# Linear attention and a gated FFN, 16 blocks of tokens: the first and last block's transpose moved from TensorE to VectorE squares and DMAs, with three steps reordered around it

## The chip, the cores and the metric

One core of a Trainium2 chip. The time is device microseconds of one execution. Beside the times there is one profiled execution, and its trace is what the profile views below come from. All clock times in this document (for example "44.55") are microseconds from the start of the span of the kernel that is named.

## What is computed

The input x is 4 x 2048 tokens of 256 features, float32. An attention without softmax, in chunks of 32 tokens, is followed by a gated FFN with integer weights; each is added to its input, and each sum is normalized.

```python
Q, K, V = x @ W_q.T, x @ W_k.T, x @ W_v.T
S = einsum('bncd,bnkd->bnck', Qc, Kc) * mask        # chunks of 32 tokens; decay ** (i - j) below the diagonal
O = einsum('bnck,bnkd->bncd', S, Vc).reshape(B, T, D)
out = sigmoid(x @ W_g.T) * O @ W_o.T + x
h = layernorm(x + out)
u = silu(h @ wg.T) * (h @ wu.T)                     # wg, wu, wd: integers / 127; hidden size 768
result = layernorm(h + u @ wd.T)
```

## The kernel before, in words

The 8192 tokens are cut into 16 blocks of 512 (`NB` = 16, `TB` = 512); a block has 4 groups (`NG`) of 128 tokens. A block goes through these steps, each a function:

- `attn_gate` (L295), `attn_y` (L311), `attn_v` (L327): products with weights from xT, the input with features on partitions. y is x times W_q.T W_k, so that scores are y times x. ScalarE takes the gate's sigmoid (L308) and copies v (L343); VectorE copies y (L324).
- `attn_scores` (L348): scores of chunks, masked by VectorE (L366); `attn_values` (L371): scores times v, times the gate (L384, goT).
- `attn_out` (L411): product with W_o (L396, tile pa), residual (L417), and `layer_norm` (L276): moments (L261, L262) and scaling (L281 to L285) on VectorE, the root (L270) on ScalarE. The result h is multiplied by 2**23 (`H_UP`).
- The transpose of h to features on partitions, as a float32r high part (hT_hi) and a float16 rest (hT_lo). Two ways exist. `transpose_h` (L425) does it on TensorE: 8 transposes of 128x128 into two PSUM banks (L433, tile pt), a ScalarE activation for the high part (L436), a VectorE operation for the rest (L437). `move_h` (L444) transposes 32x32 squares on VectorE (L451, tile sq, 4 instructions) and moves the squares to their places with 16 DMAs of 32 KB on the sync engine's queue SP (L457, tile hT); `split_h` (L465) then makes the two parts from SBUF, on ScalarE (L474) and VectorE (L475), kept in program order on their engines.
- `ffn_up` (L482): six chunks of 128 hidden units. A chunk is 8 matmuls of 512 columns into two banks (L492, tiles fg and fu); in even chunks the high parts go first, in odd ones the low parts. Then ScalarE's sigmoid s (L500), two VectorE products (L501, L503, tile u), and u split into u_hi on ScalarE (L510) and u_lo on GpSimd (L511).
- `ffn_down` (L513): 48 matmuls for a block (L396, tile fdn), 12 for each group of tokens, a high and a low part for each of six chunks; residual (L518). `finish` (L530) normalizes and stores.

Blocks 0 and 1 start the pipeline. In the loop (L569), turn b does the attention of block b + 2 and the FFN of block b: y, gate, v and scores of b + 2; `move_h` of block b + 1; three chunks of the FFN of b; the values of b + 2; `split_h` of b + 1; three more chunks; `attn_out` of b + 2; `ffn_down` of b. So blocks 1 to 14 are transposed by squares and DMAs, with a turn's work between the move and the first use. Block 0 and block 15 use `transpose_h`: block 0 before the loop (L564), block 15 in the tail after the loop (L604), in the middle of block 14's FFN. After the loop come block 14's FFN and block 15's, the latter in two halves of 256 tokens so that its end is short.

The engines work through their queues in order. A scheduler fixes these orders when the program is built, from the program's order, its own estimates and the buffers: eight PSUM banks in rotation, two buffers for most working tiles, and one each for sq and hT (the pool `moved`), so that a block's squares wait until the former block's DMAs have read theirs.

Of the kernel before, what the change touches and what calls it, by code (L numbers as in the profile page):

```python
# [48 lines left out]
TB = 512  # L49
NG = TB // P  # L50
SCALE = 1.0 / 127.0
EXACT = 2048.0
H_UP = 2.0**23
# [5 lines left out]
def kernel(  # L59
# [25 lines left out]
    work = ctx.enter_context(tc.tile_pool(name="work", bufs=2))  # L85
# [8 lines left out]
    def bank(name):  # L94
        return psum.tile([P, TB], F32, tag="ps", name=name)
# [180 lines left out]
    def layer_norm(dst, r, name, on_r=1.0, on_dst=1.0):  # L276


        mv = moments(r, name)
        rstd = root(mv, name, on_r)  # L280
        nc.vector.reciprocal(rstd, rstd)  # L281
        if on_dst != on_r:
            nc.vector.tensor_scalar(rstd, rstd, on_dst / on_r, None, ALU.mult)  # L283
        for g in range(NG):
            nc.vector.tensor_scalar(  # L285
                dst[:, g, :],
                r[:, g, :],
                mv[:, g, 0:1],
                rstd[:, g : g + 1],
                ALU.subtract,  # L290
                ALU.mult,
            )
# [55 lines left out]
    def attn_scores(b, yT):  # L348
        xt = xTs.pop(b)
        halves = [slice(i * PAIR, (i + 1) * PAIR) for i in range(P // PAIR)]  # L350
        ps = bank(f"ps_{b}")[:, : NG * PAIR].rearrange("p (g c) -> p g c", c=PAIR)
        for g in range(NG):
            for fc in range(KD):
                for rows in halves:
                    tokens = slice(g * P + rows.start, g * P + rows.stop)
                    nc.tensor.matmul(  # L356
                        ps[rows, g, :],
                        lhsT=xt[:, fc, tokens],
                        rhs=yT[:, fc, tokens],
                        start=(fc == 0),  # L360
                        stop=(fc == KD - 1),
                    )
# [45 lines left out]
    def flat(t, gs):  # L408
        return t[:, gs, :].rearrange("p g d -> p (g d)")

    def attn_out(b, goT, up=H_UP):  # L411
        xn = xns.pop(b)
        r = norm.tile([P, NG, D], F32, tag="h", name=f"h_{b}")

        def residual(gs, pb):

            nc.vector.scalar_tensor_tensor(  # L417
                flat(r, gs), flat(xn, gs), 2.0, pb, ALU.mult, ALU.add
            )

        project_back(b, (chunked(goT),), wo, KD, residual, "pa")
        layer_norm(r, r, f"a{b}", on_dst=up)
        return r

    def transpose_h(b, h, up=H_UP):  # L425

        up = H_UP / up
        hi = work.tile([P, KD, TB], F32R, tag="hT_hi", name=f"hT_hi_{b}")
        lo = work.tile([P, KD, TB], F16, tag="hT_lo", name=f"hT_lo_{b}")
        for dc in range(KD):  # L430
            pt = bank(f"pt_{b}_{dc}")
            for g in range(NG):
                nc.tensor.transpose(  # L433
                    pt[:, g * P : (g + 1) * P], h[:, g, dc * P : (dc + 1) * P], ident
                )
            nc.scalar.mul(hi[:, dc, :], pt, up)  # L436
            nc.vector.scalar_tensor_tensor(  # L437
                lo[:, dc, :], pt, up, hi[:, dc, :].bitcast(F32), ALU.mult, ALU.subtract
            )
        return hi, lo  # L440

    NQ = P // SQ

# [104 lines left out]
    goT = attn_values(first, sT, v, sg)  # L548
    if second:
        sT_second = attn_scores(second, ys.pop(second))  # L550
    hs[first] = attn_out(first, goT, 1 if NB == 1 else H_UP)
    fg, fu = (
        [integers(w, name, dtype) for dtype in (F32R, F16)]
        for w, name in zip(ffn_int, ("fg", "fu"))
    )
    if second:
        goT = attn_values(second, sT_second, v_second, sg_second)
    if NB > 2:
        xTs[2] = load_xT(2)
        ys[2] = attn_y(2)  # L560
    if second:
        hs[second] = attn_out(second, goT, 1 if NB == 2 else H_UP)
    fd = integers(ffn_int[2], "fd", F32R)
    hTs[first] = transpose_h(first, hs[first], 1 if NB == 1 else H_UP)  # L564


    half = range(KH // 2), range(KH // 2, KH)
    looked = 0
    for b in range(NB - 2):  # L569
        n = b + 2  # L570
        if n not in xTs:
            xTs[n] = load_xT(n)
        xns[n] = load_xn(n)
        hT = hTs.pop(b)
        uT = [], []
        yT = ys.pop(n) if n in ys else attn_y(n)
        sg, v = attn_gate(n), attn_v(n)
        sT = attn_scores(n, yT)
        moving = move_h(b + 1, hs[b + 1])
        ffn_up(b, hT, uT, half[0])  # L580
        goT = attn_values(n, sT, v, sg)
        hTs[b + 1] = split_h(b + 1, moving)
        ffn_up(b, hT, uT, half[1])
        hs[n] = attn_out(n, goT, 1 if n == NB - 1 else H_UP)
        finish(b, ffn_down(b, uT, hs.pop(b)))
        if looked < len(halves):
            look_up(looked)
            looked += 1
# [12 lines left out]
    if NB > 1:  # L601
# [192 lines left out]
```

## Time and profile before

| | us |
|---|---|
| three runs | 554.58, 554.70, 552.32 (median 554.58) |
| profiled execution | 552.7 |
| its span, first to last instruction | 550.9 |
| granted TensorE clock, mean | 0.997 |
| TensorE busy | 541.8 (98% of the span) |
| VectorE, ScalarE, GpSimd busy | 385.7, 230.1, 128.7 |
| one turn of the loop (75.32 to 108.72) | 33.40 |
| 8 transposes on TensorE in the chain, twice | 0.87 each time |
| 16 DMAs of a move, first issue to last issue's end (50.45 to 60.78) | 10.33 |

A line of the timeline reads: start, length, engine, line of the code, operation, output <- inputs, shapes, number of instructions merged; in brackets the idle time of the engine before it and what ended that. The chain of waits goes back from the last instruction, at each step to what released it, or to the instruction before it on its engine; its rows are start, length, engine and line. A list of waits has the engine and line that waited, the one waited for, and the total, the number and the longest of the waits. The trace's stages: start of the pipeline to about 53, then 14 turns to about 509, then the tail; the last matmuls of the FFN's chunks end near 538, and normalization and stores take the rest.

### The profile page before, as it was taken

The page shows a single profiled execution, that of the slowest core. Times are in us where ns is not written, and L with a number is a line of the kernel's source. Part 1 is how long each engine was busy: PE and PEld are TensorE (multiplying, and loading weights), DVE is VectorE, ACT ScalarE, POOL GpSimd, SP SyncE. Part 2 cuts the span into 40 slices and gives each one's busy share as a digit, 9 for nine tenths or more (in the row PEclk, how much of TensorE's full clock was granted, in tenths as well). Part 3 has the DMA queues.
Part 4 walks back from the last instruction along what each step waited for, and adds up shares of the span by engine and source line. Part 5 has one row for each costly group of instructions (what it writes and reads, how often), then busy time and mean ns, then how long its engine had stood idle before and what let it go on. Part 6 is the DMA issues. An engine that isn't in the chain of part 4 may idle for free.

```text
span 550.9 us, 8470 instructions
## 1 busy us (share of the span) xinstructions
PE 541.8 (98%) x3150; PEld 396.6 (72%) x3150; DVE 385.7 (70%) x956; ACT 230.1 (42%) x382; POOL 128.7 (23%) x122
## 2 busy tenths in 40 slices
PE   8999999999999999999999999999999999999994
PEld 5577777867668686677857778676676866778694
DVE  4276885859668486894848758496784858848874
ACT  2226524335243352533435243452433425344755
POOL 2000402205022040311305022050221403123453
PEclk9999999999999999999999999999999999999998
DMA  8431223121221312214121231213213120020102
GB/s 266 161 109 52 65 60 95 39 73 43 90 64 39 97 53 65 56 44 111 39 66 50 75 80 39 75 42 93 61 39 91 63 62 16 6 72 1 38 2 80
DMA packets 41996, 36.77 MB, mean 67 GB/s; under 512 B 4576, under 2 KB 37344, under 8 KB 41952
## 3 DMA queue, kind: packets, MB, share of 16 engines
q1 hardware_dynamic: 40832, 35.15, 22.2%
q10 hardware_dynamic: 1088, 1.05, 0.6%
q8 instruction: 26, 0.43, 0.3%
q14 instruction: 18, 0.15, 0.1%
q0 software_dynamic: 32, 0.00, 0.0%
HBM read 20.45 MB, written 8.39 MB: 52 GB/s over the span
## 4 chain that ended last, share of the span: by engine, by line
PE 97%; DMA 1%; ACT 1%; DVE 1%; issue 0%; POOL 0%; DVEq 0%
PE fg L492 16%; PE fu L492 16%; PE fdn L396 16%; PE pa L396 10%; PE pv L336 10%; PE pg L301 10%; PE py L317 10%; PE po L377 5%; PE ps L356 3%; DMA wg<-in_w_gT_dram 1%; ACT r L635 0%; PE pt L433 0%; PE pm L159 0%; ACT L270 0%; ACT rstd_f L270 0%
## 5 line engine op out<-in xcount | busy, mean ns | idle before, releaser
L511 POOL TENSOR_TENSOR u_lo<-u,u_hi 128x512 fp32r<-128x512 f32 (+1 forms) x102 | 123.9, 1216 | 412.1 <-ACT u_hi L510 407.7
L500 ACT ACTIVATE s<-fg 128x512 f32<-128x512 f32 (+1 forms) x102 | 58.1, 570 | 76.9 <-PE fg L492 76.9
L396 PE MATMUL fdn<-fd_hi,u_hi 128*128 128x256 f32 x360 | 89.1, 290 | 0.0
L396 PE MATMUL fdn<-fd_hi,u_lo 128*128 128x256 f32 x360 | 86.5, 282 | 0.0
L501 DVE TENSOR_TENSOR s<-fg,s 128x512 f32<-128x512 f32 (+1 forms) x102 | 66.7, 654 | 27.7 <-ACT s L500 27.6
L510 ACT CAST u_hi<-u 128x512 fp32r<-128x512 f32 (+1 forms) x102 | 60.4, 592 | 48.2 <-DVE u L503 48.1
L503 DVE TENSOR_TENSOR u<-fu,s 128x512 f32<-128x512 f32 (+1 forms) x102 | 67.3, 660 | 13.6 <-POOL u_lo L511 1.0
L492 PE MATMUL fg<-hT_hi,fg_hi 128*128 128x512 f32 (+1 forms) x204 | 71.4, 431 | 0.0
L366 DVE TENSOR_TENSOR sT<-ps,mask 64x256 f32<-64x256 f32 x32 | 13.5, 422 | 79.9 <-PE ps L356 79.7
L396 PEld LDWEIGHTS fdn<-fd_hi,u_lo 128*128 128x128 f32 x360 | 67.9, 189 | 0.4
L396 PEld LDWEIGHTS fdn<-fd_hi,u_hi 128*128 128x128 f32 x360 | 67.8, 189 | 0.4
L492 PE MATMUL fu<-hT_hi,fu_hi 128*128 128x512 f32 (+1 forms) x204 | 61.5, 382 | 0.0
L492 PE MATMUL fg<-hT_lo,fg_lo 128*128 128x512 f16 (+1 forms) x204 | 58.7, 369 | 0.0
L336 PEld LDWEIGHTS pv<-wv,xT 128*128 128x128 f32 x256 | 48.6, 190 | 13.4 <-issue 7.7
L492 PE MATMUL fu<-hT_lo,fu_lo 128*128 128x512 f16 (+1 forms) x204 | 58.1, 366 | 0.0
L301 PE MATMUL pg<-xT,wg 128*128 128x512 f32 x128 | 57.6, 593 | 0.3 <-DMA wg<-in_w_gT_dram 0.3
L396 PE MATMUL pa<-wo,goT 128*128 128x256 f32 x256 | 58.0, 379 | 0.0
L336 PE MATMUL pv<-wv,xT 128*128 128x256 f32 x256 | 57.9, 379 | 0.0
L317 PE MATMUL py<-xT,m_sb 128*128 128x512 f32 x128 | 57.6, 593 | 0.0
L396 PEld LDWEIGHTS pa<-wo,goT 128*128 128x128 f32 x256 | 48.5, 190 | 7.6 <-DVE rstd_a L283 0.2
L301 PEld LDWEIGHTS pg<-xT,wg 128*128 128x128 f32 x128 | 24.2, 190 | 31.0 <-issue 25.6
L492 PEld LDWEIGHTS fg<-hT_hi,fg_hi 128*128 128x128 f32 x204 | 36.6, 189 | 10.3
(90 smaller groups left out, 625.2 us busy)
## 6 DMA issues: line engine op xcount, KB each, us to landing
x<-in_x_dram SPq DMA_DIRECT2D x16, 512.0 KB, 3.6
xT<-in_xT_dram SPq DMA_DIRECT2D x15, 512.0 KB, 3.9
out_dram<-r SPq DMA_DIRECT2D x15, 512.0 KB, 3.3
hT<-sq SPq DMA_DIRECT2D x224, 32.0 KB, 1.9
fg_int<-in_ffn_gT_dram SPq DMA_DIRECT2D x1, 768.0 KB, 9.2
fu_int<-in_ffn_uT_dram SPq DMA_DIRECT2D x1, 768.0 KB, 10.6
fd_int<-in_ffn_dT_dram SPq DMA_DIRECT2D x1, 768.0 KB, 11.0
xT<-in_xT_dram SPq DMA_DIRECT2D x2, 256.0 KB, 4.4
```

Source lines behind the costliest of these rows:

```text
L301: nc.tensor.matmul(pg, lhsT=wg[:, ec, dc * P : (dc + 1) * P], rhs=xt[:, ec, :], start=(ec == 0), stop=(ec == KD - 1),)
L317: nc.tensor.matmul(py, lhsT=m_sb[:, ec, fc * P : (fc + 1) * P], rhs=xt[:, ec, :], start=(ec == 0), stop=(ec == KD - 1),)
L336: nc.tensor.matmul(pv[:, j * D : (j + 1) * D], lhsT=xt[:, ec, g * P : (g + 1) * P], rhs=wv[:, ec, :], start=(ec == 0), stop=(ec == KD - 1),)
L356: nc.tensor.matmul(ps[rows, g, :], lhsT=xt[:, fc, tokens], rhs=yT[:, fc, tokens], start=(fc == 0), stop=(fc == KD - 1),)
L377: nc.tensor.matmul(po[:, cols], lhsT=v[:, g, dc * P : (dc + 1) * P], rhs=sT[:, cols], start=True, stop=True,)
L396: nc.tensor.matmul(pb[:, j * D : (j + 1) * D], lhsT=part[k][:, g * P : (g + 1) * P], rhs=w[:, k, :], start=(i == 0), stop=(i == len(terms) ...
L492: nc.tensor.matmul(pb, lhsT=w[kind][:, dc, hc * P : (hc + 1) * P], rhs=hT[kind][:, dc, cols], start=(kind == kinds[0] and dc == 0), stop=( ...
L500: nc.scalar.activation(s, pg, AF.Sigmoid, scale=SCALE / H_UP)
L501: nc.vector.tensor_tensor(s, pg, s, ALU.mult)
L503: nc.vector.tensor_tensor(u, pu, s, ALU.mult)
L510: nc.scalar.copy(hi, u)
L511: nc.gpsimd.tensor_tensor(lo, u, hi.bitcast(F32), ALU.subtract)
```

## The change

`transpose_h` goes, and with it the option of `attn_out` to leave h unscaled: every block's h carries the factor 2**23 and is transposed by `move_h` and `split_h`. Around this:

- Block 0: `move_h` right after its `attn_out`; `split_h` in the first turn, after the scores of block 2.
- The input xT of block 3 is loaded with that of block 2, and block 3's y is made in the first turn, between the scores of block 2 and the first chunk of block 0's FFN, no longer in block 1's turn.
- Block 1: `split_h` after all six chunks of block 0's FFN, no longer in their middle.
- Block 15: in the last turn (b = 13), `attn_out` is done after four chunks of block 13's FFN instead of six (the variable `late` holds the other two), then `move_h` of block 15, the two late chunks, the first two chunks of block 14's FFN (`ahead`), and then block 13's `ffn_down`. In the tail come chunks 2 to 4 of block 14, a ScalarE multiplication that takes the factor out of block 15's h (128x1024), `split_h` of block 15, and chunk 5.

```diff
-    def attn_out(b, goT, up=H_UP):
+    def attn_out(b, goT):
...
-        layer_norm(r, r, f"a{b}", on_dst=up)
+        layer_norm(r, r, f"a{b}", on_dst=H_UP)
...
-    def transpose_h(b, h, up=H_UP):
...
-    hs[first] = attn_out(first, goT, 1 if NB == 1 else H_UP)
+    hs[first] = attn_out(first, goT)
+    moving = move_h(first, hs[first])
...
+    for b in range(2, min(NB, 4)):
+        xTs[b] = load_xT(b)
     if NB > 2:
-        xTs[2] = load_xT(2)
         ys[2] = attn_y(2)
...
-    hTs[first] = transpose_h(first, hs[first], 1 if NB == 1 else H_UP)
...
+    ahead = half[0][: 2 if NB > 2 else 0]
+    uTs = {}
...
-        hT = hTs.pop(b)
-        uT = [], []
+        uT = uTs.pop(b, ([], []))
         yT = ys.pop(n) if n in ys else attn_y(n)
         sg, v = attn_gate(n), attn_v(n)
         sT = attn_scores(n, yT)
+        if b == first:
+            hTs[b] = split_h(b, moving)
+            if n + 1 < NB:
+                ys[n + 1] = attn_y(n + 1)
+        hT = hTs.pop(b)
         moving = move_h(b + 1, hs[b + 1])
         ffn_up(b, hT, uT, half[0])
         goT = attn_values(n, sT, v, sg)
-        hTs[b + 1] = split_h(b + 1, moving)
-        ffn_up(b, hT, uT, half[1])
-        hs[n] = attn_out(n, goT, 1 if n == NB - 1 else H_UP)
+        if b != first:
+            hTs[b + 1] = split_h(b + 1, moving)
+
+        late = half[1][1:] if n == NB - 1 else half[1][:0]
+        ffn_up(b, hT, uT, half[1][: len(half[1]) - len(late)])
+        if b == first:
+            hTs[b + 1] = split_h(b + 1, moving)
+        hs[n] = attn_out(n, goT)
+        if n == NB - 1:
+            moving = move_h(n, hs[n])
+            ffn_up(b, hT, uT, late)
+            uTs[b + 1] = [], []
+            ffn_up(b + 1, hTs[b + 1], uTs[b + 1], ahead)
         finish(b, ffn_down(b, uT, hs.pop(b)))
...
-        uT = [], []
-        ffn_up(last - 1, hTs[last - 1], uT, half[0])
-        hTs[last] = transpose_h(last, hs[last], 1)
-        ffn_up(last - 1, hTs[last - 1], uT, half[1])
+        uT = uTs.pop(last - 1, ([], []))
...
+        ffn_up(last - 1, hTs[last - 1], uT, range(len(ahead), KH - 1))
+        plain = flat(hs[last], slice(0, NG))
+        nc.scalar.mul(plain, plain, 1 / H_UP)
+        hTs[last] = split_h(last, moving)
+        ffn_up(last - 1, hTs[last - 1], uT, range(KH - 1, KH))
```

More of the change, by code (lines that the diff above doesn't have):

```diff
@@ L421, in attn_out @@
         project_back(b, (chunked(goT),), wo, KD, residual, "pa")
-        layer_norm(r, r, f"a{b}", on_dst=up)
+        layer_norm(r, r, f"a{b}", on_dst=H_UP)
         return r
-    def transpose_h(b, h, up=H_UP):
[L427 to L440, printed above, removed]
     NQ = P // SQ
@@ L557 @@
         goT = attn_values(second, sT_second, v_second, sg_second)
+    for b in range(2, min(NB, 4)):
+        xTs[b] = load_xT(b)
     if NB > 2:
-        xTs[2] = load_xT(2)
         ys[2] = attn_y(2)
     if second:
-        hs[second] = attn_out(second, goT, 1 if NB == 2 else H_UP)
+        hs[second] = attn_out(second, goT)
     fd = integers(ffn_int[2], "fd", F32R)
-    hTs[first] = transpose_h(first, hs[first], 1 if NB == 1 else H_UP)
     half = range(KH // 2), range(KH // 2, KH)
+    ahead = half[0][: 2 if NB > 2 else 0]
+    uTs = {}
     looked = 0
@@ L600 @@
     early = range(0)
-    if NB > 1:
-        uT = [], []
-        ffn_up(last - 1, hTs[last - 1], uT, half[0])
-        hTs[last] = transpose_h(last, hs[last], 1)
-        ffn_up(last - 1, hTs[last - 1], uT, half[1])
+    if NB == 1:
+        hTs[last] = split_h(last, moving)
+        plain = flat(hs[last], slice(0, NG))
+        nc.scalar.mul(plain, plain, 1 / H_UP)
+    else:
+        uT = uTs.pop(last - 1, ([], []))
+        if NB == 2:
+            hTs[last - 1] = split_h(last - 1, moving)
+            moving = move_h(last, hs[last])
+        ffn_up(last - 1, hTs[last - 1], uT, range(len(ahead), KH - 1))
+        plain = flat(hs[last], slice(0, NG))
+        nc.scalar.mul(plain, plain, 1 / H_UP)
+        hTs[last] = split_h(last, moving)
+        ffn_up(last - 1, hTs[last - 1], uT, range(KH - 1, KH))
         early = half[0]
```

## The prediction

> **What bounds the kernel now.** I read the busy shares first, then who waits, then the chain of waits, at both ends of the span. The page's first part and the chain's shares:
>
> ```profile
> PE 541.8 (98%) x3150; PEld 396.6 (72%) x3150; DVE 385.7 (70%) x956; ACT 230.1 (42%) x382; POOL 128.7 (23%) x122
> ...
> PE 97%; DMA 1%; ACT 1%; DVE 1%; issue 0%; POOL 0%; DVEq 0%
> ```
>
> TensorE is the bound in every stage but the last 13 us. TensorE's list of waits has two rows, both at the start:
>
> ```profile
> PE pi L145 <- DVE idle L142: 1.5, 1, 1.5
> PE pg L301 <- DMA wg<-in_w_gT_dram: 0.3, 1, 0.3
> ```
>
> So nothing in the middle can be won by shortening a wait: a gain needs TensorE work to go, and any new wait of TensorE is a loss of its full length. The work that goes, in the chain (start, length):
>
> ```profile
> 41.09 3.45 PE pa L396 x16
> 44.55 0.87 PE pt L433 x8
> 45.42 3.44 PE pg L301 x8
> 48.86 3.45 PE pv L336 x16
> 52.31 1.08 PE ps L356 x32
> ...
> 514.58 0.87 PE pt L433 x8
> ```
>
> What replaces it is the path by which blocks 1 to 14 already go. In the timeline, the first such move (block 1):
>
> ```profile
> 47.70 1.38 DVE L285 TENSOR_SCALAR h<-h,mv_a,rstd_a 128x256 f32<-128x256 f32 x4
> 49.00 1.42 DVE L451 STREAM_TRANSPOSE sq<-h 128x256 f32<-128x256 f32 x4
> 50.45 10.33 SPq L457 DMA_DIRECT2D hT<-sq  x16
> 62.07 1.14 ACT L474 CAST hT_hi<-hT 128x512 fp32r<-128x512 f32 x2 [0.68 <-DMA hT<-sq]
> ```
>
> The reader is to see 11.65 us from the end of the transposes (50.42) to the first hT_hi (62.07), 10.3 of it the issue of 16 DMAs one behind the other. A TensorE transpose takes 0.87; this takes 13 with the squares. It is free only under 13 us of other TensorE work.
>
> **What the Trainium skill says.** "VectorE: DVE Perf Modes", section "The three transpose paths": only TensorE and the DMA crossbar do a full 128x128; VectorE does 32x32 blocks, hence the DMAs. It gives 390 ns for one on TensorE (bf16); here eight f32 ones add 870 ns to the chain, 109 each. [...]the trace has 1.9 us median from issue to landing (1.8 to 3.6). "ScalarE: Activation LUTs", "What ACT_TABLE_LOAD costs": 1283 ns plus a drain of 1380. The trace has 1.28, and the next operation starts 0.01 later (539.47 to 540.76), so I use 1.28 alone. "TensorE: Matmul & The Clock Gate", Part 1: the clock falls after an idle window of some 3.4 us; the granted clock is 0.997 here, and no wait below is that long, so I add nothing for it.
>
> **The change part by part.** The instruction queues of the built program agree with the ones before from block 1's turn to the middle of block 13's (block 3's y apart): only the two ends change. Times are in the clock of the profiled execution before.
>
> *Removed:* 16 transposes, 2 x 0.87 = 1.74 us, all on the path.
>
> *Start.* Block 2's gates now start at 44.55, so gates, v and scores end at 44.55 + 3.44 + 3.45 + 1.08 = 52.52. Block 3's y (3.43) stands there now instead of in block 1's turn: its cost is moved, not added. Block 0's first chunk may start at 55.95. Its data: the normalization L285 of block 0 starts at 40.43; as in the rows above, transposes start 1.30 later and last 1.42, so 43.15; plus 11.65 is 54.80; two casts at 0.53 to 0.6 give hT_hi at 55.4 and 55.95, just in time. ScalarE, with an additional pair of table loads between the two gate sigmoids (2 x 1.28), is free at 54.25 by its queue: covered by 0.5. VectorE decides. The buffer of the squares is single, so block 1's squares wait for block 0's 16 DMAs (54.80), and three of them (1.07) and a copy of y (0.65) are queued ahead of hT_lo: 56.5, then 0.65 each, 57.15 and 57.8. TensorE wants hT_lo at 55.95 + 2 x 0.47 = 56.9 and would be through with the gate's low pair at 57.35; now 57.8 + 0.22 = 58.0. **New wait S = 0.7.** From both sides: 0 if the DMAs are issued at the 0.585 that is the shortest in the trace (0.9 earlier), 2.4 if the last lands after 3.6 instead of 1.9. No gain is possible, since the work is unchanged.
>
> On SP's queue the 16 DMAs pass ahead of block 3's x (about 53.6 instead of 45.3; it is read some 50 us later) and of block 4's xT: nothing. Block 1's own move starts near 59.4 and lands near 71; its chunks start near 87: 16 us of cover. In block 1's turn TensorE has 3.43 less work ahead of block 2's split: landing some 15 us after the down projection, read at 16; only ScalarE would wait, and the next reader on TensorE is a turn away. Nothing.
>
> *End.* A chunk is 1.80 (three in 60.77 to 66.17). Block 15's output product moves from 499.95 to 496.35, ending 499.80; its goT is ready at 495.73, covered by 0.6. Then follow chunks 4 and 5 of block 13 (to 503.40), chunks 0 and 1 of block 14, and the down projection of block 13 from 507.1. The rows before for its last chunk's cover:
>
> ```profile
> 501.29 0.69 DVE L503 TENSOR_TENSOR u<-fu,s 128x512 f32<-128x512 f32 x1
> ...
> 502.01 0.62 ACT L510 CAST u_hi<-u 128x512 fp32r<-128x512 f32 x1 [0.80 <-DVE u L503]
> ...
> 502.71 1.29 POOL L511 TENSOR_TENSOR u_lo<-u,u_hi 128x512 fp32r<-128x512 f32 x1
> ```
>
> After the chunk's matmuls (499.95) the low part is ready at 504.0, used at 504.56. Now block 15's normalization and four transposes stand ahead of chunk 5 on VectorE: residual and moments 499.05 to 502.3 (3.25, as at 468.55), chunk 4's two products to 503.8, reciprocal and scaling to 504.15, normalization and squares 1.30 + 1.42 to 506.87, then s of chunk 5, s of the next, u of chunk 5: 508.75. Cast 0.62, GpSimd 1.29: high part 509.4, low part 510.7. The program has put these two terms at places 18 and 23 of the projection, at 0.12 each: wanted at 509.15 and, 0.6 later, 510.0. **New wait A = 1.0**; 0 if VectorE's queue runs 1 us shorter, 2.5 if the terms stood in their old places (11 and 12) or the queue is 1.5 longer. The rescaling of h (128x1024; an estimate of 1.1, twice a 128x512 activation of 0.59) ends near 508.0 on ScalarE, 0.75 ahead of the cast.
>
> Let E be the projection's end. Block 15's DMAs, from 506.9, land near 518.5; E is about 513.9 and its split comes at E + 6.5: covered by 1.9. But the split's VectorE half stands behind chunk 4 of block 14. Before, the second chunk after the projection had its u at 515.56, E + 6.39 (two table loads, block 13's normalization and chunk before it). So now chunk 3's u is at E + 6.4, chunk 4's at E + 7.8, hT_lo at E + 9.05 and 9.65. TensorE has four chunks, 7.2 us, and 0.46 of high parts: it wants hT_lo at E + 7.66. **New wait B = 1.5**, from 0.5 to 2.6 (two VectorE products more or fewer). Then chunk 5's u, behind two products, is at E + 11.35, its low part at E + 13.3; block 14's projection starts at E + 7.2 + 1.5 + 2.75 (three half chunks, 520.85 to 523.60) = 11.45 and wants it eleven matmuls later, 12.8: **C = 0.5**, from 0 to 1. The last 13 us are as before.
>
> **Sum:** -1.74 + 0.7 + 1.0 + 1.5 + 0.5 = **+2.0 us**. Span 550.9 to 552.9; the profiled execution 552.7 to 554.7. The three runs before are 552.32, 554.58 and 554.70, so executions fall near 552.5 or near 554.6; I add 2.0 to the mean of all four, 553.6: **555.6**. Against the median of 554.58 that is within 0.5%, which is about what a measurement of this kernel can tell from no change.
>
> **The rivals.** *The covers hold* (chance 0.22): hT_lo and u_lo come as fast as the shortest rows allow, waits total 0.7 or less: -1.0, 552.6. For it: each wait hangs on less than 1.5 us. Against: VectorE is 89% busy from 500 to 521 already (18.71 of 21.00), and its order is fixed. *VectorE at the end becomes the bound* (0.28), and it ends slower: normalization, squares and split of block 15 all lie in VectorE's queue ahead of products that TensorE needs, so A, B and C near their upper ends, 2.5 + 2.6 + 1.0, with S 0.7: 6.8 - 1.7 = +5.1, 558.7. It decides from 4.5 us of waits on (1.74 + 2.77). *The change doesn't do it*: the queues show the transposes gone; no chance given. The forecast has 0.50.
>
> **How the numbers follow.** More than 0.5% faster would be 2.8 us, and only 1.74 can be won: 0.03, for the spread of runs alone. Slower by over 0.5%: the second rival, 0.28. The rest, 0.69. The range 552.6 to 558.4 leaves out half of the first rival and a part of the second.
>
> **What would show it.** In the profile after: no pt rows; TensorE waits of about 0.7 near 57 (on hT_lo), 1.0 near 510 (on u_lo, GpSimd), 1.5 near 521 (on hT_lo), 0.5 near 526 (on u_lo); nothing between. I am wrong if these total under 1 or over 4.5, if TensorE waits for a DMA, or if the middle blocks' 33.4 us turn changes.

## The result and the profile after

The changed kernel takes 560.81 us (median of 5 runs, 558.7 to 561.5), the kernel before 553.22 in the same comparison: ratio 1.0129, 95% interval 1.0102 to 1.0156. It is 7.6 us slower, and above the range that was forecast. The profiled execution is the fastest of the five: 558.7, span 556.9, against 552.7 and 550.9 before. So the trace explains 6.0 us of the 7.6; the rest comes back under e6.

The page's first part and the chain's shares, of the changed kernel:

```profile
PE 543.8 (98%) x3134; PEld 396.4 (71%) x3134; DVE 390.8 (70%) x965; ACT 236.2 (42%) x387; POOL 129.2 (23%) x122
...
PE 90%; DVE 4%; ACT 2%; SPq 2%; DMA 1%; issue 1%; POOL 1%; DVEq 0%
```

The 16 transposes are gone (3150 matmuls to 3134), and yet TensorE is busy 2.0 us longer. A matmul that runs at half clock counts as busy (the table of windows below shows it), so this row hides a loss. In the chain TensorE's share falls from 97% to 90%: other engines now set its pace. Its list of waits:

```profile
PE fg L475 <- DVE hT_lo L458: 2.9, 4, 1.9
PE pi L145 <- DVE idle L142: 1.5, 1, 1.5
PE fdn L396 <- POOL u_lo L494: 0.9, 2, 0.5
PE fdn L396 <- ACT u_hi L493: 0.2, 1, 0.2
```

These waits are on the named tiles, 4.0 us in all without the warm-up. Three of the four forecast waits are among them: near 57, near 510 and, later than forecast, at 524.7. One of the two waits for u_lo, 0.38 us at 104.77, was not forecast. The rest of the loss has to be found by milestones. I take five from TensorE's timelines: the start of the first output product (32.15 before), of block 5's output product (166.09), of block 15's down projection (537.66), its end (543.63), and the end of the span (550.9). Each stage's entry is how much longer it is than before, in us. The span is read to 0.1 us, so the last two columns are good to 0.1:

| kernel | median us | ratio to before, interval | to first product | blocks 0 to 5 | to last projection | after its end | span |
|---|---|---|---|---|---|---|---|
| changed kernel | 560.81 | 1.0129 [1.0102, 1.0156] | 0.10 | 0.67 | 4.87 | 0.37 | 6.0 |
| e1_start_alone | 554.52 | 1.0028 [1.0019, 1.0038] | 0.45 | 0.53 | -0.07 | 1.20 | 2.1 |
| e2_end_alone | 559.87 | 1.0125 [1.0109, 1.0141] | 0.67 | 0.07 | 5.36 | 1.20 | 7.3 |
| e3_no_overlap | 556.69 | 1.0071 [1.0056, 1.0085] | 0.00 | 0.36 | 2.89 | 1.16 | 4.4 |
| e4_filled | 559.45 | 1.0116 [1.0098, 1.0134] | 0.80 | 0.41 | 4.42 | 1.27 | 6.9 |
| e5_split_early | 556.14 | 1.0047 [1.0033, 1.0062] | -0.50 | 0.43 | 2.20 | 1.37 | 3.5 |
| e6_turn1_late | 560.32 | 1.0128 [1.0111, 1.0145] | -0.12 | 0.02 | 6.48 | 1.12 | 7.5 |
| e7_small_first | 565.30 | 1.0228 [1.0196, 1.0259] | 6.12 | 0.53 | 4.73 | 0.03 | 11.4 |
| e8_all_earlier | 559.96 | 1.0116 [1.0098, 1.0134] | 0.48 | -0.03 | 5.46 | 1.40 | 7.3 |
| e9_two_edits | 556.11 | 1.0052 [1.0033, 1.0071] | -0.31 | -0.04 | 2.17 | 1.39 | 3.2 |
| e10_two_buffers | 555.08 | 1.0038 [1.0028, 1.0048] | -0.50 | -0.81 | 2.18 | 1.23 | 2.1 |
| e11_start_mended | 553.04 | 0.9997 [0.9985, 1.0008] | 0.79 | -0.81 | -0.07 | 1.10 | 1.0 |
| e12_squares_behind | 555.87 | 1.0055 [1.0037, 1.0072] | -0.42 | -0.05 | 2.73 | 0.54 | 2.8 |
| e13_warm_pieces | 559.87 | 1.0128 [1.0104, 1.0152] | 0.68 | 0.03 | 5.45 | 1.34 | 7.5 |
| e14_start_mended_warm | 552.00 | 0.9987 [0.9978, 0.9995] | -0.37 | -0.81 | -0.06 | -0.16 | -1.4 |
| e15_mended_warm | 554.99 | 1.0039 [1.0026, 1.0052] | -0.61 | -0.81 | 2.18 | 1.15 | 1.9 |

Each row's stages are of one profiled execution. Before the first product, executions differ by -0.6 to 0.8 us with no difference in TensorE's work (e7 and the cut warming matmuls of e13 to e15 apart); the traces show the full clock granted first between 4.3 and 7.5 us, and mostly the later it is, the later the first product. So a change of half a microsecond is read from a stage, not from a single total.

The loss has three places: the end of the middle (block 15's split), block 1's turn, and the stores at the very end.

**Block 15's split.** VectorE's timeline of the changed kernel:

```profile
522.52 0.69 DVE L486 TENSOR_TENSOR u<-fu,s 128x512 f32<-128x512 f32 x1
523.13 3.23 DVE L458 TENSOR_TENSOR hT_lo<-hT,hT_hi 128x512 f16<-128x512 f32 x2
```

The projection of block 13 ends at E = 514.71. u of chunk 4 starts at 522.52, E + 7.8, as forecast; but the two hT_lo behind it take 3.23 us. Two of them take 1.28 where GpSimd makes no u_lo beside them, and 1.97 in 13 of the 14 turns before, where it makes one (a row of these stands under block 1's turn). GpSimd in the same microseconds makes two:

```profile
522.87 2.94 POOL L494 TENSOR_TENSOR u_lo<-u,u_hi 128x512 fp32r<-128x512 f32 x2 [0.75 <-ACT u_hi L493]
```

TensorE waits 1.91 us, to 524.73, and 0.45, to 526.41. Then its clock, in the table of windows (window, its length, TensorE busy and instructions, granted clock, DMA share, GB/s):

```profile
523.00:524.00 1.00, 0.00 (x0) 1.00 0.00 0
524.00:525.00 1.00, 0.27 (x2) 0.87 0.00 0
525.00:526.00 1.00, 0.96 (x5) 0.50 0.00 0
526.00:527.00 1.00, 0.59 (x4) 0.50 0.00 0
527.00:528.00 1.00, 1.00 (x6) 0.50 0.00 0
528.00:529.00 1.00, 1.00 (x10) 0.93 0.00 0
```

From 524.7 to 528.1 the granted clock is half. The matmuls of 256 columns start 0.21 us apart there, against 0.11 at full clock in e4 below; yet apart from the second wait, in the row of 526, they count as busy.

**Block 1's turn.** VectorE after, and then ScalarE after:

```profile
97.14 1.29 DVE L458 TENSOR_TENSOR hT_lo<-hT,hT_hi 128x512 f16<-128x512 f32 x2 [1.75 <-ACT hT_hi L457]
```

```profile
96.49 1.14 ACT L457 CAST hT_hi<-hT 128x512 fp32r<-128x512 f32 x2 [1.64 <-DMA hT<-sq]
```

In the kernel before, the same hT_lo starts 1.84 us earlier and waits for nothing; below it the u_lo that runs beside it:

```profile
95.30 1.97 DVE L475 TENSOR_TENSOR hT_lo<-hT,hT_hi 128x512 f16<-128x512 f32 x2
94.82 1.30 POOL L511 TENSOR_TENSOR u_lo<-u,u_hi 128x512 fp32r<-128x512 f32 x1 [0.42 <-ACT u_hi L510]
```

Chunks 3 to 5 of block 1 queue behind it on VectorE. On ScalarE chunk 3's sigmoid stands behind the cast hT_hi: its gate's matmuls were through at 95.6, it starts at 97.54. The projection, from 102.7 on, waits for chunk 5's low part and takes 6.70 us instead of 6.11.

### The profile page after: what moved, and what is told of

It reads as the page before. It is cut to its first block, busy times and chain, and to the rows that moved or that the text cites. A ratio compares the mean times of both kernels' runs of the same rounds, so it can differ in the third digit from the quotient of the medians.

```text
span 556.9 us, 8508 instructions
## 1 busy us (share of the span) xinstructions
PE 543.8 (98%) x3134; PEld 396.4 (71%) x3134; DVE 390.8 (70%) x965; ACT 236.2 (42%) x387; POOL 129.2 (23%) x122
## 4 chain that ended last, share of the span: by engine, by line
PE 90%; DVE 4%; ACT 2%; SPq 2%; DMA 1%; issue 1%; POOL 1%; DVEq 0%
PE fg L475 15%; PE fdn L396 15%; PE fu L475 14%; PE pg L301 9%; PE pv L336 9%; PE py L317 9%; PE pa L396 9%; PE po L377 5%; PE ps L356 3%; SPq L440 2%; DVE u L486 1%; PE pi L145 1%; DVE sq L434 1%; DVE hT_lo L458 1%; DMA out_dram<-r 1%
## 5 line engine op out<-in xcount | busy, mean ns | idle before, releaser
L475 PE MATMUL fg<-hT_hi,fg_hi 128*128 128x512 f32 (+1 forms) x204 | 73.1, 438 | 0.0
```

What stands on the lines that cost most here:

```text
L475: nc.tensor.matmul(pb, lhsT=w[kind][:, dc, hc * P : (hc + 1) * P], rhs=hT[kind][:, dc, cols], start=(kind == kinds[0] and dc == 0), stop=( ...
```

## The experiments

Theories at this point. *Cover*: the end costs most, because the split of block 15 has one chunk in front of it and its hT_lo are slow beside GpSimd; the clock follows from the wait. Its first rival: the start costs most. Others stand with each run. The stages in what follows are those of the table.

**Start alone and end alone.** e1: `transpose_h` and the old order for block 15, the rest of the change kept.

```diff
-        if n == NB - 1:
-            moving = move_h(n, hs[n])
-            ffn_up(b, hT, uT, late)
...
-        hTs[last] = split_h(last, moving)
+        hTs[last] = transpose_h(last, hs[last], 1)
```

> Only the start of the change: block 0's h goes by squares and DMAs and block 3's y stays moved; block 15 is transposed by TensorE as in the kernel before, and the last output product stays behind all six chunks. Theory (the loss is made at the end, at block 15's split): -0.87 for eight transposes, +0.8 for block 0's late low part, +0.65 for the late split of block 2 in block 1's turn, so +0.6 us on the kernel before, ratio 1.001; TensorE's waits at the end are those of the kernel before. Rival (the start costs most of the loss, through S at its upper end of 2.4 and the turn after it): +3 us or more, ratio 1.005 or more.

Measured: 1.0028, +1.6 us. The first five blocks cost 0.53, as expected, the end nothing; but 1.20 us more pass after the last projection, which no theory had.

e2: `transpose_h` for block 0, no moved y, the change's end.

> Only the end of the change: block 15's h goes by squares and DMAs and the last output product stands ahead of two chunks; block 0 is transposed by TensorE and block 3's y stays in its turn, as in the kernel before. Theory: -0.87 for eight transposes, A 1.1, B 4.4, C 0.2, tail 0.4, so +5.2 us on the kernel before, ratio 1.009; TensorE waits about 1.9 and 0.45 us for hT_lo, and its granted clock falls after that. Rival (the start makes most of it): +2 us, ratio under 1.004.

Measured: 1.0125, +7.0 us; the end stage 5.36, and again 1.20 after it. The loss is made at the end; the first rival falls.

**Is hT_lo slow because of GpSimd?** e3 takes the two overlapping u_lo off GpSimd:

```diff
+            if b == NB - 2 and hc in (KH - 3, KH - 2):
+                waiting_lo.append((lo, u, hi))
+                continue
             nc.gpsimd.tensor_tensor(lo, u, hi.bitcast(F32), ALU.subtract)
...
+        for lo, u, hi in waiting_lo:
+            rest = nc.vector.tensor_tensor(lo, u, hi.bitcast(F32), ALU.subtract)
+            tc.keep_in_program_order(rest)
```

> The whole change, but GpSimd's low parts of chunks 3 and 4 of block 14 are made by VectorE behind block 15's split, so that GpSimd does nothing while the two hT_lo run. Theory (the two hT_lo ran at 1.65 us each in place of 0.69 because GpSimd's u_lo ran beside them): each takes 0.69, the second ends 2.0 us earlier, TensorE waits 1.4 to 1.6 us in one piece in place of 1.91 and 0.45, and the time falls by about 2 us against the changed kernel, a little more if the clock holds: 558.7 to 556.5 in the profile. Rival (they are slow for their operands: hT read out of order just after the DMAs, or the order of their access): they stay at 1.6 to 1.75 us and the time stays or grows by the two operations added to VectorE.

VectorE's timeline of e3:

```profile
522.71 1.28 DVE L458 TENSOR_TENSOR hT_lo<-hT,hT_hi 128x512 f16<-128x512 f32 x2
```

and a row of TensorE's waits:

```profile
PE fg L477 <- DVE hT_lo L458: 1.6, 3, 1.0
```

The same two operations on the same data take 1.28 us instead of 3.23. TensorE's longest wait is 1.0, the clock stays at 1.00, and the time falls from 1.0129 to 1.0071, by 4.1 us, where 2 were expected; the trace's end stage falls by 2.0 (the changed kernel's trace is its fastest execution). The rival (slow operands) falls. The Trainium skill names this contention: "GPSIMD Engine Reference", section "1. Specifications", has the SBUF interfaces shared with VectorE, with contention for VectorE instructions that have two SBUF inputs. hT_lo is one (hT and hT_hi). That section gives no size; here the two took 1.55 and 1.75 us instead of 0.68 each, and GpSimd's two u_lo 2.94 instead of 2.53 (at 510.01, with no hT_lo beside them).

The single operations show more than a slowing. In the changed kernel the first u_lo ends at 524.14, and the hT_lo that had begun beside it at 524.68; the second u_lo, begun at 524.09, ends only at 525.80, 1.12 us behind that hT_lo, and the second hT_lo at 526.36, again 0.55 behind it. In all 17 traces 248 hT_lo made from SBUF began while a u_lo was running, and 246 of them ended 0.54 to 0.55 us behind that u_lo's end, whatever was left of it; the other 284 took 0.68 to 0.69. So of the two operations the later one is held until the earlier is through. The products u, which have one input in PSUM, took 0.69 us beside a u_lo and without one. In the kernel before, block 15's hT_lo read its first input from PSUM too (tile pt): the one at 517.96 took 0.68 us in the midst of a u_lo (517.27 to 518.56). It was the move to SBUF that opened block 15's split to this hold.

**Is it the wait that slows the clock?** e4 fills the two waits with matmuls that nobody reads (`product` is one of the FFN's matmuls of chunks 0 and 1):

```diff
+        def fill(n):
+            for _ in range(n):
+                in_turn(
+                    nc.tensor.matmul(
+                        spare,
+                        lhsT=fg[0][:, 0, :P],
+                        rhs=hT[0][:, 0, :],
...
+        for dc in range(KD):
+            fill(fills[dc])
+            for hc in (0, 1):
+                for which in (0, 1):
+                    product(hc, which, 1, dc)
...
+        filled(last, hTs[last], cols[0], (8, 3))
         ffn_up(last, hTs[last], uT_last, early, cols[0])
```

> The whole change, with eight and three matmuls of 128x512 that nobody reads put where TensorE waits for the two hT_lo (1.91 and 0.45 us); they leave their sums in a spare bank, nothing of the output is changed. Theory of the clock (TensorE's half speed from 524.7 to 528 us follows from its idling in that wait): granted clock stays at 1.0 through the wait, the matmuls of 256 columns behind it stand 0.11 us apart in place of 0.21, and block 14's projection starts about 0.9 us earlier: the time falls by 0.9 us against the changed kernel. Rival (the clock falls for another reason, or is only shown so): no change within 0.2 us, and the spacing stays 0.21 us; if the added matmuls run beyond the wait the time grows by what runs over.

Windows of e4:

```profile
525.00:526.00 1.00, 1.00 (x8) 1.00 0.00 0
526.00:527.00 1.00, 0.61 (x5) 1.00 0.00 0
```

The two hT_lo took as long as in the changed kernel (3.28 us), the clock stayed at 1.00, and matmuls of 256 columns stood 0.11 us apart. The end stage is 4.42, against 4.73 to 6.48 in the five kernels with the same end and no filling (changed kernel, e2, e6, e7, e13), though only four of these five fell to half clock; from the last hT_lo to block 14's projection 1.8 us pass instead of 2.5. The median fell by 1.4 us, which the intervals alone don't separate from nothing; the clock and the spacing do.

What settles it is a count over all 17 traces. Every change of the granted clock lies a whole multiple of 3.413 us behind the first full clock of its trace, so the clock is decided in windows of that length. Behind the first 20 us, each window at full clock in which TensorE idled 1.90 us or more was followed by half clock, and none with 1.86 or less. In the changed kernel the window up to 524.74 held all 1.91 us of the wait; in e7 the same wait of 1.91 was cut by the end of a window (1.35 us of idle in one, 1.53 in the next), and the clock stayed. So the fall follows from idling, and whether a wait of two microseconds brings it depends on where the windows lie.

In e7 block 14's projection starts 0.8 us sooner behind E than in the changed kernel, and then takes 6.82 us instead of 6.15, waiting for a low part. So one period of half clock costs the end stage little (4.87 in the changed kernel, 5.36 in e2 and 5.45 in e13, against e7's 4.73 without one).

**More cover.** e5 moves one call:

```diff
-        ffn_up(last - 1, hTs[last - 1], uT, range(len(ahead), KH - 1))
+        ffn_up(last - 1, hTs[last - 1], uT, range(len(ahead), KH - 2))
...
         hTs[last] = split_h(last, moving)
-        ffn_up(last - 1, hTs[last - 1], uT, range(KH - 1, KH))
+        ffn_up(last - 1, hTs[last - 1], uT, range(KH - 2, KH))
```

> The whole change with block 15's split one chunk of the FFN earlier: behind chunk 3 of block 14 in place of chunk 4, ahead of two chunks in place of one. Theory (B is a lack of cover: two hT_lo at 1.65 us each beside GpSimd, one chunk of 1.7 us in front of them, then half speed of the clock behind the wait): the last DMA lands near 520.5 us, both hT_lo are done by 523.5 at the latest, TensorE waits under 0.4 us, its clock stays at 1.0, and block 14's projection starts 3 to 4 us earlier than in the changed kernel; 560.8 goes to about 556.5. Rival (the squares' DMAs land too late for the earlier place, so that VectorE and ScalarE wait in their turn and the chunks behind are late): gain under 1.5 us.

Measured: 556.14, 4.7 us less than the changed kernel, as the theory said. Two rows of its waits:

```profile
PE fdn L396 <- POOL u_lo L494: 1.2, 3, 0.6
PE fg L475 <- DVE hT_lo L458: 0.8, 3, 0.3
```

The longest wait for hT_lo is 0.3 and the clock stays full. But the end stage is still 2.20: what is left is A and a new C, since block 14's projection now comes sooner and takes 7.20 us, waiting for low parts, where it took 5.99 in the kernel before. The earlier place also missed the second u_lo: the two hT_lo take 1.56 us here. So e5 doesn't tell how much of its gain is more cover and how much a shorter hold.

**Block 1's turn.** In e6 block 2's split comes behind all six chunks:

```diff
-        if b != first:
+        if b > 1:
             hTs[b + 1] = split_h(b + 1, moving)
...
-        if b == first:
+        if b <= 1:
             hTs[b + 1] = split_h(b + 1, moving)
```

> The whole change, but in block 1's turn the split of block 2 stands behind all six chunks, as the change has it in block 0's turn, in place of behind three. Theory (in block 1's turn the DMAs of block 2's h land 1.8 us after VectorE is free for hT_lo, since the moved y no longer stands ahead of the FFN; chunks 3 to 5 queue behind it and the projection waits for chunk 5's low part): the wait in that turn goes and everything behind is 0.3 to 0.6 us earlier; the end stays as it is, the time falls by 0.5 us. Rival (that difference comes from somewhere else in the turn): no change within 0.2 us at the start of the third projection.

Measured: the stage from the first product to block 5 falls from 0.67 to 0.02, as the theory said. By itself that is weak, for e13, which leaves the split in its place, shows 0.03 too; but in the four kernels with this edit and one buffer (e6, e8, e9, e12) the stage is 0.02 or less, and in the seven others with the changed start it is 0.03 to 0.67. The total hardly moves (560.32), because the clock did worse in this execution:

```profile
527.00:528.00 1.00, 1.00 (x6) 0.50 0.00 0
530.00:531.00 1.00, 1.00 (x6) 0.50 0.04 8
```

Half speed lasts from 524.5 to 531.3, 6.8 us, twice as long as in the changed kernel's trace; the end stage is 6.48. So the same wait brings no such period (e7), one or two: in e6 the second wait, 0.96 us, fell into the half-speed window, and the next one was at half speed too. With two the end stage is 1.0 to 1.6 us longer than with one. The changed kernel's four other executions have no trace, but their mean granted clock, 0.989 to 0.991 against 0.993 in the profiled one, is like e6's (0.988 to 0.992) and fits a second period in some of them. That, and the 0.7 to 1 us that most traces have more after the last projection, is enough for the 1.6 us by which the median loss exceeds the trace's.

**All three at once.** e8 joins e5 and e6, and puts block 15's values and output product one chunk earlier (three late chunks):

```diff
-        ffn_up(b, hT, uT, half[0])
+        head = half[0][:-1] if n == NB - 1 else half[0]
+        ffn_up(b, hT, uT, head)
         goT = attn_values(n, sT, v, sg)
+        ffn_up(b, hT, uT, half[0][len(head) :])
...
-        late = half[1][1:] if n == NB - 1 else half[1][:0]
+        late = half[1] if n == NB - 1 else half[1][:0]
```

> Three edits of the changed kernel together: block 15's split one chunk earlier; in block 13's turn block 15's attention values and output product one chunk earlier too, so that three chunks stand between that product and block 13's projection; block 2's split behind all six chunks of block 1. Theory: A (1.1), B with the clock (4.4 to 5.5) and block 1's wait (0.5) go; 560.8 goes to about 554, and with the two transposes' 1.74 gone and block 0's late low part left at 0.8 it ends near the kernel before, ratio 0.999 to 1.003. Rival (VectorE is the bound of the end, so that what is taken from one place is waited for at the next): two thirds of the loss at most are won back, 556 or more.

Measured: 559.96, 0.9 us won back where 6.8 were expected: the rival was right here. The wait moved from B to A:

```profile
PE fdn L396 <- ACT u_hi L493: 2.4, 1, 2.4
```

GpSimd, VectorE and ScalarE in e8 show why:

```profile
504.46 2.51 POOL L494 TENSOR_TENSOR u_lo<-u,u_hi 128x512 fp32r<-128x512 f32 x2 [5.72 <-ACT u_hi L493]
504.64 1.13 DVE L283 TENSOR_SCALAR rstd_a<-rstd_a 128x4 f32<-128x4 f32 x1
505.80 2.29 DVE L285 TENSOR_SCALAR h<-h,mv_a,rstd_a 128x256 f32<-128x256 f32 x4
...
511.23 0.62 ACT L493 CAST u_hi<-u 128x512 fp32r<-128x512 f32 x1 [0.71 <-DVE u L486]
```

Chunk 5's sigmoid is done by 507.1, but its products on VectorE start at 509.35 only, behind the scaling and the squares of block 15. Two steps of that scaling met u_lo: L283 took 1.13 us (0.17 in e9), L285 2.29 for its four (1.38 in e9), and each held operation ended within 0.15 us behind a u_lo. These 1.9 us are most of the wait of 2.4; that reading is from the trace, no run takes the two u_lo away. Moving the product earlier moved this block of work beside two u_lo and just ahead of what TensorE needs next, and the wait again halved the clock. e5's edit is good, the earlier product is not: e9, without it, has a ratio of 1.0052 against 1.0116.

**Both good edits, then two buffers, then the squares later.** e9 is e5 and e6:

> The whole change with two edits: block 15's split one chunk earlier (556.14 alone) and block 2's split behind all six chunks of block 1. Theory: the two waits are apart, so both savings add: 0.65 us less than the first edit alone, 555.5; TensorE's only waits left at the end are those for chunk 5's parts at block 13's projection (A, 0.7 in the waits) and under 0.4 for hT_lo, and the granted clock stays at 1.0 there. Rival (they share a cause, as a lower clock over the whole run): no gain on 556.1.

Measured: 556.11, no less than e5. The stages do add (blocks 0 to 5: -0.04 after 0.43; end 2.17 after 2.20); the median doesn't resolve the half microsecond. e10 gives the squares and hT two buffers:

```diff
-    moved = ctx.enter_context(tc.tile_pool(name="moved", bufs=1))
+    moved = ctx.enter_context(tc.tile_pool(name="moved", bufs=2))
```

> The same two edits, and two buffers each for the squares and for the transposed h in place of one, so that block 1's squares need not wait for block 0's sixteen DMAs. Theory (S: block 0's low part stands on VectorE behind those squares): hT_lo of block 0 is made right behind its high part, TensorE's two waits of 0.30 and 0.22 us in the first FFN go, and the time falls by 0.5 to 0.8 us: 554.9. Rival (block 0's DMAs land too late by themselves): under 0.2 us.

Measured: 555.08; blocks 0 to 5 fall by another 0.77. VectorE in the changed kernel, with one buffer, and below it in e10:

```profile
55.00 1.10 DVE L434 STREAM_TRANSPOSE sq<-h 128x256 f32<-128x256 f32 x3 [1.48 <-DMA hT<-sq]
56.73 1.28 DVE L458 TENSOR_TENSOR hT_lo<-hT,hT_hi 128x512 f16<-128x512 f32 x2
```

```profile
55.01 1.29 DVE L458 TENSOR_TENSOR hT_lo<-hT,hT_hi 128x512 f16<-128x512 f32 x2 [0.36 <-ACT hT_hi L457]
```

So S is in the main what the single buffer cost, as the prediction had it. e12 is e9 with block 15's squares behind the two late chunks:

```diff
-            moving = move_h(n, hs[n])
             ffn_up(b, hT, uT, late)
+            moving = move_h(n, hs[n])
```

> The two edits, with block 15's squares and DMAs behind chunks 4 and 5 of block 13 in place of ahead of them. Theory (A comes from the squares, 1.4 us of VectorE in front of chunk 5's s and u, and there is no slack for them anywhere): A goes (1.1 us), but the DMAs start 1.3 us later, so the split is late by about 2 us counted from block 13's projection, TensorE waits for hT_lo again, and the time is 1 us longer or more than with the two edits. Rival (there is slack behind the landing): A's 1.1 is a gain, 554.4.

Measured: 555.87, the same as e9. The scheduler put two of the four squares behind chunk 5's products, and chunk 5's low part was ready 2.42 us into block 13's projection instead of 3.67 (e9), about as the theory had it. But the program now reads it at place 12 of the projection, as in the kernel before, and in e9 at place 23; TensorE waits 0.97 us for it, and A stays at 1.0 (7.13 us for the projection, 7.07 in e9). For the later hT TensorE waited only 0.35 and 0.14 us. So A depends on the place that the scheduler gives the term as much as on VectorE; the earlier low part, read at place 23 as in e9, was not tried.

**The 1.2 us after the last projection.** In all kernels of the table but the changed kernel itself, e7, e12 and e14, the third of the last four stores takes over 1.1 us to issue, and the last waits behind it. SP's rows for these four, in the kernel before, e11 and e14 (minimum, median, maximum ns):

```profile
L650 SPq DMA_DIRECT2D out_dram<-r x4: 332/338/345, 545.4 to 547.9; - x4
```

```profile
L665 SPq DMA_DIRECT2D out_dram<-r x4: 345/364/1457, 545.2 to 548.3; - x4
```

```profile
L667 SPq DMA_DIRECT2D out_dram<-r x4: 332/338/345, 544.1 to 546.6; - x4
```

In the trace of each kernel with such a late store, a transfer of kind "instruction" on queue 8 starts with the third of them or up to 0.35 us ahead of it, 2.9 to 3.2 us behind the end of the last projection. In the changed kernel's own trace and in e12 it starts at 3.4 to 3.5, past the third store, and only the fourth is late, 0.66 and 0.69 us; in the kernel before it starts at 1.7. The queue has 26 such transfers of 16,384 bytes in the kernel before, one for some 250 records of TensorE, so I took them for TensorE's instructions. Several runs test it. e7 puts matmuls of one column in front of everything:

```diff
+    for _ in range(16):
+        nc.tensor.matmul(pi[:, :1], lhsT=idle[:, :P], rhs=idle[:, :1], start=True, stop=True)
```

> The whole change with 16 matmuls of one column in front of everything, in TensorE's first wait; nobody reads them. They only move every later instruction of TensorE by 16 places in its program. Theory (the last four stores are sometimes 1.2 to 1.6 us to issue in place of 0.34 because an instruction fetch on queue 8 falls beside them, 3 us behind TensorE's last matmul in the changed kernel and 1.7 us in the kernel before; the fetch follows TensorE's program): the fetch moves by some 1.7 us to the front, no issue of the last four takes over 0.4 us, and the time from TensorE's end to the span's end is 7.3 us; against the other kernels with the whole change about 0.5 to 1 us shorter there. Rival (the fetch follows another engine's program, or time alone): the long issue stays.

Measured: the fetch now comes 0.5 us ahead of the projection's end, no store takes over 344 ns, and that stage is 0.03. The rest of e7 was a surprise: 6.1 us more before the first product (below). e11 is e1 with e6's edit and two buffers. e13 is the whole change, e14 is e11 and e15 is e10, each with the warming matmuls cut in pieces (diff below):

> Only the start of the change (block 15 by TensorE and the last output product in its old place), with block 2's split behind all six chunks and with two buffers. Theory: block 1's wait (0.5) and S (0.5 to 0.8) go, 0.87 for eight transposes stays: TensorE's last projection starts 0.6 to 0.9 us earlier than in the kernel before; if the stores at the end are issued as in the other changed kernels (one of four over 1.2 us), 1 us of that is lost again, and the ratio is 0.999 to 1.001. Rival (the start can't be mended, VectorE is late there anyway): ratio 1.002 or more, as with the start alone.

> The whole change with TensorE's two warming matmuls of 512 columns cut into four of 128 and two of 256: the same columns, eight more matmul records and as many weight loads in TensorE's program, nothing else. Theory (the last four stores are late in the changed kernels because an instruction fetch on queue 8, which follows TensorE's program, now falls beside them): every fetch comes some 1.5 to 2 us earlier counted from TensorE's work, no store of the last four takes over 0.4 us to issue, and from the end of the last projection to the end of the span it is 7.3 us, as in the kernel before, in place of 8.4 to 8.7 us; the time falls by about 1 us. Rival (the fetch follows time or another engine): one of the four stores stays at 1.2 us or more and the time is the same.

> Only the start of the change, mended (block 2's split behind six chunks, two buffers), with the warming matmuls in pieces. Theory: what the mended start won, 0.9 us at the last projection, was given back by the late stores; without them the time is 0.9 to 1.1 us under the kernel before, ratio 0.998. Rival: ratio 1.000, as without the pieces.

> The whole change with block 15's split one chunk earlier, block 2's behind six chunks, two buffers, and the warming matmuls in pieces. Theory: 555.1 less 1.1 for the stores, 554.0; ratio 1.0015 to 1.003; what is left is A and C, TensorE's waits for low parts in the last two blocks' projections. Rival: 555.1.

```diff
-    for _ in range(WARM):
-        nc.tensor.matmul(pi, lhsT=idle[:, :P], rhs=idle, start=True, stop=True)
+    for n in (TB // 4,) * 4 + (TB // 2,) * 2:
+        nc.tensor.matmul(pi[:, :n], lhsT=idle[:, :P], rhs=idle[:, :n], start=True, stop=True)
```

e11: the mended start wins 0.81 in its stage and loses 1.10 after the last projection: ratio 0.9997. e14: the fetch comes 1.0 us behind the last projection, no late store, that stage is -0.16, and the kernel is at 552.0, ratio 0.9987 (0.9978 to 0.9995): a little faster than both kernels. e13 and e15: the first three fetches came 1.3 to 2.3 us earlier counted from the first product, but the last one, counted from the last projection, did not, and the late store stayed. So a late store and the fetch go together over 17 traces, and in the two where the fetch was moved away (e7, e14) the stores were on time; but what places the last fetch isn't only the number of TensorE's instructions, and stays open.

e13 also shows a part of block 1's turn. There block 2's 16 DMAs and the store among them took 11.8 us to issue (82.93 to 94.76), in the changed kernel 12.6 (82.33 to 94.90), where a fetch met the store and made it 1.50 long. Counted from the first product, e13's last issue ends 0.7 us earlier, and the turn lost nothing (0.03). So the 0.65 hangs on less than a microsecond of SP's queue, behind a move that starts 3 us later than before.

## Why the prediction was wrong, point by point

- *Removed, -1.74*: right. *S = 0.7*: at block 3's output product the changed kernel is level with the kernel before (+0.02, the first product's 0.10 taken off), so S was 0.89; two buffers gave 0.77 of it back.
- *Block 1's turn, "only ScalarE would wait, and the next reader on TensorE is a turn away. Nothing."*: wrong, 0.65. I had given the landing one microsecond of slack; it came late, and the cast and hT_lo stand in program order on ScalarE and VectorE, ahead of chunks 3 to 5. So ScalarE waited 1.64 us and VectorE 1.75 with them, and those chunks feed TensorE in the same turn: a wait of ScalarE alone was not free either.
- *A = 1.0*: right. Block 13's projection took 7.08 us, 6.12 before, and TensorE waited at the two places named, 18 and 23 (e12 shows how much hangs on the place).
- ***B = 1.5***: the step that failed most; it measured 4.4. From E to block 14's projection 14.13 us passed; before it was 14.19, with two more chunks (3.6) and the transposes (0.87), so 9.7 without a wait. "hT_lo at E + 9.05 and 9.65" rests on 0.65 us for each, which holds only with no u_lo beside them; they ended at E + 10.0 and E + 11.65. "Block 14's projection starts at ... 11.45" became E + 14.13: 2.7 later, 2.0 because hT_lo was held by u_lo (3.23 for 1.28) and 0.7 from the clock (2.5 us from the last hT_lo to the projection instead of 1.8, as in e4). My bound of 2.6 took "two VectorE products more or fewer", but never a longer one, although in the trace before the pair took 1.97 us in 13 of 14 turns, one of them up to 1372 ns beside a u_lo.
- *The clock: "no wait below is that long, so I add nothing for it"*: wrong. The Trainium skill, "TensorE: Matmul & The Clock Gate", Part 1, has a free-running window of 3413 ns and an idle window before the clock falls. The length agrees: half speed lasted 3.4 us (524.7 to 528.1) or 6.8. But TensorE had been idle only 1.9 of the 3.4 us ahead of the fall; so a window idle in part is enough here (1.90 us or more of 3.41, in the count above), and the measurement decides. One wait of 1.0 (e3) did it no harm. For the total the clock weighs less than the hold: 0.1 to 0.7 us in the end stage with one period, some 1.0 to 1.6 more with a second.
- *C = 0.5*: 0.16 (the projection of block 14 took 6.15, 5.99 before), with B in front of it; without B, in e5, it is 1.2.
- *"The last 13 us are as before"*: 0.4 more behind the last projection in the profiled execution, 1.0 to 1.4 in most other traces, through a late store.
- *The base of 553.6*: 0.4 too high for the median of 553.22 here, and no cause of the miss.

Sum in the trace: 0.10 + 0.67 + 4.87 + 0.37 = 6.0, against 2.0. The second rival (VectorE at the end becomes the bound, 558.7) had the place, but A and C did not go to their ends; B went beyond its own, through two causes that it didn't name. That its 558.7 is also the time of the profiled execution is chance. My test "wrong if these total over 4.5" would not have rung: the waits total 4.0, since half speed and slow stores are in no row of waits.

## What to carry to other kernels

A duration taken from a row holds for the neighbours it had there. Before pricing a VectorE operation with two SBUF inputs, look which GpSimd operations will run beside it, and price the hold: here what was left of the u_lo, and 0.55 us behind its end. The longest of the row is no bound (1.37 us before, 1.75 after, where two u_lo stood in a row). When TensorE's wait is priced, add what can follow it: here 1.9 us of wait brought up to 6.8 us at half clock, which shows as busy time and in no list of waits. And an operation held in program order makes everything behind it on its engine late, so "its own reader comes a turn later" is no proof that its wait is free.

## What the runs showed of the hardware

The windows of e7, which begins with 32 records of one-column matmuls from 4.7 us on:

```profile
4.00:6.00 2.00, 2.00 (x15) 1.57 (x13) 0.00 (x0) 0.09 (x1) 0.27 (x1) 1.00 0.66 240
...
8.00:10.00 2.00, 2.00 (x6) 1.41 (x7) 1.90 (x18) 0.00 (x0) 0.00 (x0) 0.50 1.05 389
```

TensorE is busy 2.00 of 2.00 us with them, yet its clock falls to 0.50 at 7.8 and stays there for 6.8 us. The first output product is 6.1 us late: 3.4 of it because the gate's first matmul starts at 8.59 instead of 5.21, behind the added ones, the rest with the half clock. In this run matmuls of one column did not keep the clock up; in e4 matmuls of 512 columns did. An SP issue that met an instruction transfer of queue 8 took up to 1.9 us instead of 0.33 to 0.6, in the middle as at the end; behind the first 10 us no trace has an issue of over 0.9 us without such a transfer beside it.
